# Selective scan of a two-layer convolution net: one scan instruction for two states, loops swapped, half sums kept, background work placed in half slots

## The chip, the cores and the metric

The kernel runs on one core of one Trainium2 chip, in float32 throughout. The metric is device microseconds of one launch, as a median over runs. The host only lays the arrays out.

## The reference, cut to what matters

Two layers, each added to its own input after a group norm. Layer 0 is a row recurrence (a masked convolution along a row and a gated state carried from row to row). Layer 1 takes each image of 96 channels through a wavelet split into 64x64 bands; the low band goes through a two-dimensional selective scan, the high bands through a channel attention, and a transposed convolution joins them again. The change lies in the selective scan:

```python
x_dbl = jnp.einsum('bkdl,kcd->bkcl', xs, x_proj_w)
dts, Bs, Cs = jnp.split(x_dbl, [DT_RANK, DT_RANK + D_STATE], axis=2)
delta = jax.nn.softplus(jnp.einsum('bkrl,kdr->bkdl', dts, dt_w) + dt_b[None, :, :, None])
A = -jnp.exp(A_logs).reshape(K, D_INNER, D_STATE)
def step(hst, inp):
    u_t, d_t, B_t, C_t = inp
    dA = jnp.exp(d_t[..., None] * A)
    hst = dA * hst + (d_t * u_t)[..., None] * B_t[:, :, None, :]
    y = jnp.einsum('bkdn,bkn->bkd', hst, C_t)
    return (hst, y)
```

There are 8 images, K = 4 directions (rows, columns, and both backwards), 192 channels, 16 states and 4096 positions. For each direction, channel and state a first-order recurrence runs over the 4096 positions, and the 16 states are summed with weights C into one output.

## The kernel before, in words

**Stages.** Layer 0 and a set-up come first. Then the wavelet analysis of image 0 runs alone. Then comes the scan stage, 3072 slots in a row, in which the scans of image b have beside them, as background, the analysis of image b+1 and the output and synthesis of image b-1. The output and synthesis of image 7 run alone at the end.

**A slot.** The positions are cut into 8 chunks of 512 (`CH`). One pass `p` holds two directions: 128 partitions are 64 channels of a row direction and 64 of a column direction, and `q` = 0..2 picks the channel group. A slot is one chunk, one channel group and a pair (`GN` = 2) of states; a chunk has 24 slots, with the channel group innermost, so three slots in a row share a tile `bct` with the rows B and C of the pair, broadcast by DMA to the partitions (`load_bc`, L928). In a slot:

- POOL makes `xb` = `du` x B, 1024 elements, three slots ahead (`product`, L937).
- ACT makes `da` = exp(delta x A), two instructions of 512 elements into PSUM (`decay`, L946). There are three such one-bank buffers.
- DVE runs two scans of 512 elements over `da` and `xb` (`scan`, L953), in place in `da`; each takes its starting state from a column of the tile `carry`.
- DVE multiplies the states with C into `hc`, two instructions of 512 (L1102), and ACT copies the last state into `carry` (L1104). In every sixth slot (`by_pool`) the scan writes into `xb` instead, and POOL does the multiplication (L1096).
- PE sums over the states: transposing matmuls with the identity add each `hc` into the group's accumulator `py`, one PSUM bank for each of the three groups (`add_up`, L970). After the chunk's last pair ACT copies `py` out (L1034). In the backward pass the forward sum `yf` is loaded and added by a matmul (L1009).

**Background.** Jobs are Python generators; each step names an engine, an estimated time, a least distance in slots from the step before, and resources (PSUM banks, short tiles). `write` emits the steps that are due. In a slot the steps of SP, PE and ACT are emitted after the first `decay` and ahead of the scans; the steps of DVE and POOL are emitted at the slot's end, behind `hc`:

```python
write(left, EARLY, full)     # SP, PE, ACT
for j in range(GN):
    scan(s, j, None if first else carry)
...                          # product, hc, carry copies
write(left, LATE, full)      # DVE, POOL
```

`pin` then fixes the order of the instructions on each engine as it was emitted. Many jobs have a chain of ACT steps whose result a DVE step of least distance 0 uses, so that both fall into one slot: `softplus` (L910 to L912, then L914 on DVE), `silu` (L617 to L619, then L622), `norm` (L592, then L595; L600 and L601, then L605) and the output (L846, then L848).

**Turned tiles.** The column directions need the image transposed. `turn_u`, `turn_y` and `turn_r` collect 32 rows or columns (`HALF`), and ACT's queue then writes them to DRAM in runs of 32 elements: `turned` (L685, L686), `flush` (L1000, L1001), and `columns` (L669).

Of the kernel before, what the change touches and what calls it, by code (L numbers as in the profile page):

```python
# [7 lines left out]
F32 = mybir.dt.float32  # L8
# [15 lines left out]
HALF = 32  # L24
# [3 lines left out]
NSHORT = 12  # L28
# [28 lines left out]
def forward_kernel(ctx: ExitStack, tc: tile.TileContext, i, out):  # L57
# [172 lines left out]
    with ExitStack() as s:  # L230
# [103 lines left out]
        bcp = s.enter_context(tc.tile_pool(name="bbc", bufs=3))  # L334
        sp = s.enter_context(tc.tile_pool(name="bs", bufs=2))
        psh = s.enter_context(tc.tile_pool(name="bpsh", bufs=3, space=PSUM))
        psy = s.enter_context(tc.tile_pool(name="bpsy", bufs=1, space=PSUM))
# [33 lines left out]
        for k in range(4):  # L371
            r, p, h0 = dtrow[k], k // 2, k % 2
            nc.sync.dma_start(onecol[r + 6:r + 7, h0:h0 + 1], one)
            for q in range(3):
                ds = slice(64 * ((q + h0) % 3), 64 * ((q + h0) % 3) + 64)
                hs = slice(64 * h0, 64 * h0 + 64)
                nc.sync.dma_start(dw[r:r + 6, p, q, hs], i["dt_wT"][k, :, ds])
                nc.sync.dma_start(dw[r + 6:r + 7, p, q, hs], i["dt_b"][k, ds, :].rearrange("d o -> o d"))
                nc.sync.dma_start(av[hs, p, q, :], i["A_logs"][k, ds, :])
        nc.scalar.activation(av, av, AF.Exp)  # L380
# [52 lines left out]
        turn_u = wp.tile([128, W2, HALF], F32, name="turn_u")  # L433
        turn_y = wp.tile([128, H2, HALF], F32, name="turn_y")
        turn_r = wp.tile([128, H2, HALF], F32, name="turn_r")

# [20 lines left out]
        class Job:  # L457
# [3 lines left out]
            def __init__(self, due, gen, after=(), take=(), give=(), urgent=0):  # L461
# [12 lines left out]
        free = dict(bank=2, short=NSHORT, raw=3, ph=2, wa=2)  # L474
        jobs = []
        now = [0]
# [4 lines left out]
        def write(left, engines, full):  # L481

            moved = True
            while moved:
                moved = False
                for job in list(jobs):
                    if job.due > now[0] or not all(a.done and a.at < now[0] for a in job.after):
                        continue
# [8 lines left out]
                    while not job.done:  # L497
                        eng, us, wait, take, give = job.next
                        if eng not in engines or now[0] < job.at + wait or not takes(take):
                            break  # L500
                        if us > left[eng] and left[eng] < full[eng]:
                            break
# [11 lines left out]
        def add(due, gen, after=(), take=(), give=(), urgent=0):  # L514
            job = Job(due, gen, after, take, give, urgent)
# [7 lines left out]
        def hasten(job):  # L523
            if not job.done:
# [4 lines left out]
        def drain(until):  # L529
# [4 lines left out]
            while not all(j.done for j in until):  # L534
                big = dict(SP=1e9, PE=1e9, ACT=1e9, DVE=1e9, POOL=1e9)
                write(dict(big), EARLY, big)
                write(dict(big), LATE, big)
# [4 lines left out]
        def analysis(b, begin, end):  # L542
# [7 lines left out]
            def bands(j, g):  # L550
# [6 lines left out]
                raw = io.tile([128, 9, W], F32, name="raw", bufs=3)  # L557
# [12 lines left out]
                for ty in range(2):  # L570
                    yield "PE", 2.6, (1 if ty == 0 else 0), (BANK if ty == 0 else NONE), NONE
                    if ty == 0:
                        pd = ps.tile([128, 8, W2], F32, name="pd", tag="mm")
                    for tx in range(3):
                        nc.tensor.matmul(pd, wa[:, 3 * ty + tx, :], ph[:, ty:ty + 8, tx:tx + W2],  # L575
                                         start=(ty == tx == 0), stop=(ty == 1 and tx == 2))
                yield "ACT", 1.7, 1, NONE, BANK + ("ph", "wa")
                pdf = pd.rearrange("p r w -> p (r w)")
                his = short("his")
                nc.scalar.activation(his[0:96], pdf[0:96], AF.Copy, accum_out=part[:, g, j:j + 1])  # L580
                nc.scalar.copy(lls[32 * (g % 3):32 * (g % 3) + 32], pdf[96:128])
# [32 lines left out]
            def silu(pre, name):  # L614
                yield "ACT", 1.85, 1, NONE, NONE
                e = short("e")
                nc.scalar.activation(e, pre, AF.Exp, scale=-1.0)  # L617
                nc.scalar.activation(e, e, AF.Ln, bias=1.0)
# [5 lines left out]
            def project(j, part_i):  # L624
# [3 lines left out]
                for t0 in range(0, 9, 3):  # L628
                    yield "PE", 2.6, (1 if t0 == 0 else 0), (BANK if t0 == 0 else NONE), NONE
                    if t0 == 0:  # L630
                        pc = ps.tile([128, 8, W2], F32, name="pc", tag="mm")
                    for tap in range(t0, t0 + 3):
                        ty, tx = divmod(tap, 3)
                        nc.tensor.matmul(pc, wc[:, tap, d0:d0 + 128], xp[:, r + ty:r + ty + 8, tx:tx + W2],  # L634
                                         start=(tap == 0), stop=(tap == 8))
# [3 lines left out]
                hl = 8 * j % HALF  # L639
# [16 lines left out]
            def x_proj(odr, rhs, at):  # L656
# [9 lines left out]
                for dst, src in ((bc_d[b][odr], bcs[bp.start:bp.start + 32]),  # L666
                                 (bc_d[b][odr + 2], bcs[bp.start + 32:bp.start + 64]),
                                 (dt_d[b][dp], bcs[dp])):
                    nc.scalar.dma_start(at(dst), src if odr == 0 else src.rearrange("p (w h) -> p w h", h=HALF))  # L669
# [5 lines left out]
            def columns(half, c):  # L675
                nw = 512 // HALF
# [3 lines left out]
                    lambda d: d.rearrange("r (w h) -> r w h", h=H2)[:, nw * c:nw * c + nw, HALF * half:HALF * half + HALF])  # L680

            def turned(half):
                yield "ACT", 0.68, 1, NONE, NONE
                dst = u_d[b][1].rearrange("d (w h) -> d w h", h=H2)[:, :, HALF * half:HALF * half + HALF]
                nc.scalar.dma_start(dst[0:128], turn_u)  # L685
                nc.scalar.dma_start(dst[128:192], turn_r[0:64])  # L686

# [27 lines left out]
            def conv(j):  # L715
# [3 lines left out]
                first = list(old) if j % 4 == 0 else []  # L719
# [8 lines left out]
                if j % 4 == 3:  # L728
                    group = [p for t in range(j - 3, j + 1) for p in rows[t]]
                    td = put(at(0.65), turned(j // 4), after=group)  # L730
                    cl = [put(at(0.7 + 0.1 * c), columns(j // 4, c), after=group, take=SHORT, give=SHORT)
                          for c in range(4)]
# [446 lines left out]
```

## Time and profile before

| what | value |
|---|---|
| median of 3 runs | 16440.75 us (16437.21 to 16448.39) |
| the profiled execution: its time, its span | 16478.75 us, 16477.0 us |
| DVE busy | 12537.6 us (76% of the span) |
| PE busy, granted clock | 12192.1 us (74%), 0.842 |
| POOL busy | 10069.3 us (61%) |
| ACT busy | 8640.4 us (52%) |
| DMA: bytes, packets, packets under 512 B | 2236.11 MB, 1879932, 744738 |
| first and last scan start | 3583.2 us and 15975.5 us |

Busy times are shares of the whole span, and the stages differ: layer 0 is set by PE, the scan stage is not. "Idle before" in a group's row is the time in which that engine had nothing running just before the group's instructions, and the releaser named is what ended the wait.

### The profile page before, as it was taken

Reading aid. Unit: us, or ns where it says so; the run is one execution under the profiler, and the core shown is the slowest. Engines: PE = TensorE matmul, PEld = TensorE weight load, DVE = VectorE, ACT = ScalarE, POOL = GpSimd, SP = SyncE. Lnnn points to the kernel's source line nnn. Section 1 sums busy time; section 2 is a strip of 40 time slices with the busy share of each in tenths; the row PEclk is TensorE's granted clock in tenths of the full one; section 3 lists DMA queues with packets and bytes.
Section 4 is the critical chain, followed back from the end, with each engine's and each line's share of the span. In section 5 each row is a group of like instructions: output and inputs, shape, how many; then the busy total and the mean of one; then the engine's idle time right before and its main releaser. Section 6 shows DMA issues by size and latency. Waiting matters only on the chain. (4 is left out here: it accounts for less than half of the span.)

```text
span 16477.0 us, 148859 instructions
## 1 busy us (share of the span) xinstructions
PE 12192.1 (74%) x42082; PEld 6635.8 (40%) x42082; DVE 12537.6 (76%) x14498; ACT 8640.4 (52%) x17217; POOL 10069.3 (61%) x5752
## 2 busy tenths in 40 slices
PE   2999999577766777777777677767777677766666
PEld 1444444234444444444444444444444444434432
DVE  4333333139999988998899889988998899889971
ACT  1444444246665655565566556655655566544540
POOL 1333333028777766776677667766777677777760
PEclk9999999778877888888888888888888888877766
DMA  7333332346767776777677767767776777676653
GB/s 166 70 70 70 71 70 56 78 99 156 161 137 152 169 156 142 161 166 156 142 169 162 151 149 161 164 147 155 167 156 147 154 164 165 142 147 141 145 117 75
DMA packets 1879932, 2236.11 MB, mean 136 GB/s; under 512 B 744738, under 2 KB 944867, under 8 KB 1878852
## 3 DMA queue, kind: packets, MB, share of 16 engines
q1 hardware_dynamic: 1260611, 2004.22, 56.3%
q10 hardware_dynamic: 618496, 222.37, 6.0%
q8 instruction: 338, 5.54, 0.1%
q14 instruction: 487, 3.98, 0.1%
HBM read 1859.05 MB, written 367.00 MB: 135 GB/s over the span
## 5 line engine op out<-in xcount | busy, mean ns | idle before, releaser
L937 POOL TENSOR_TENSOR xb<-du,bct 128x1024 f32<-128x1024 f32 x3072 | 7192.7, 2363 | 2295.5 <-DMA bct<-bc_d 1893.3
L953 DVE TENSOR_TENSOR_SCAN da<-da,carry,xb 128x512 f32<-128x512 f32 x4480 | 5507.1, 1269 | 395.1 <-ACT da L946 338.9
L946 ACT ACTIVATE da<-dl,av 128x512 f32<-128x512 f32 x6144 | 4196.8, 690 | 999.2 <-DVE hc L1102 430.4
L970 PE MATMUL py<-ident,hc 128*128 128x128 f32 x20480 | 3464.1, 319 | 1595.8 <-DVE hc L1102 1582.9
L970 PEld LDWEIGHTS py<-ident,hc 128*128 128x128 f32 x20480 | 2791.5, 164 | 2925.8 <-DVE hc L1102 2509.7
L1102 DVE TENSOR_TENSOR hc<-da,bct 128x512 f32<-128x512 f32 x5120 | 3234.7, 671 | 164.6 <-PE py L970 164.3
L1104 ACT COPY carry<-da 128x1 f32<-128x1 f32 x4480 | 694.6, 155 | 3039.9 <-DVE hc L1102 2859.5
L180 PE MATMUL pg<-hx,wq 128*128 128x512 f32 x4608 | 2019.9, 592 | 0.0
L970 PE MATMUL py<-ident,xb 128*128 128x128 f32 x4096 | 760.9, 347 | 1130.3 <-POOL xb L1096 1125.6
L797 PE MATMUL pd<-ph,wg 128*128 128x504 f32 (+1 forms) x2304 | 1176.9, 657 | 308.1 <-DMA ph<-ll_d 116.5
L180 PEld LDWEIGHTS pg<-hx,wq 128*128 128x128 f32 x4608 | 871.7, 189 | 1107.0 <-issue 1106.2
L1096 POOL TENSOR_TENSOR xb<-xb,bct 128x1024 f32<-128x1024 f32 x512 | 1203.0, 2350 | 155.2 <-DVE xb L953 119.2
L575 PE MATMUL pd<-ph,wa 128*128 128x512 f32 x2304 | 1151.8, 643 | 149.8 <-DMA raw<-x_d 111.9
L970 PEld LDWEIGHTS py<-ident,xb 128*128 128x128 f32 x4096 | 616.8, 179 | 1502.3 <-POOL xb L1096 1426.9
L953 DVE TENSOR_TENSOR_SCAN xb<-da,carry,xb 128x512 f32<-128x512 f32 x896 | 1100.0, 1262 | 129.3 <-ACT da L946 96.3
L634 PE MATMUL pc<-xp,wc 97*128 97x512 f32 x2304 | 1126.7, 631 | 45.8 <-ACT attn L705 16.8
L185 ACT ACTIVATE gate<-pg,gbias 32x512 f32<-32x512 f32 x768 | 523.5, 682 | 1184.8 <-PE pg L180 1184.7
L197 POOL TENSOR_TENSOR x1b<-xb,hx 96x512 f32<-96x512 f32 x256 | 301.7, 1179 | 1372.5 <-DVE hx L196 1126.8
L191 DVE TENSOR_TENSOR gate<-gate,gate 96x512 f32<-96x512 f32 x256 | 186.6, 729 | 842.1 <-ACT gate L185 842.1
L953 DVE TENSOR_TENSOR_SCAN da<-da,xb 128x512 f32<-128x512 f32 x640 | 749.5, 1211 | 96.2 <-ACT da L946 70.6
L797 PEld LDWEIGHTS pd<-ph,wg 128*128 128x128 f32 x2304 | 470.8, 216 | 830.7 <-issue 634.8
L575 PEld LDWEIGHTS pd<-ph,wa 128*128 128x128 f32 x2304 | 460.3, 211 | 652.8 <-issue 477.0
(168 smaller groups left out, 11918.4 us busy)
## 6 DMA issues: line engine op xcount, KB each, us to landing
bct<-bc_d SPq DMA_DIRECT2D x2048, 512.0 KB
raw<-x_d SPq DMA_DIRECT2D x384, 288.0 KB
xb<-in_x SPq DMA_DIRECT2D x64, 1536.0 KB
wa<-wa_d SPq DMA_DIRECT2D x192, 384.0 KB
xs<-in_x SPq DMA_DIRECT2D x64, 1024.0 KB
x_d<-x1b SPq DMA_DIRECT2D x792, 64.0 KB
du<-u_d SPq DMA_DIRECT2D x128, 384.0 KB
yf_d<-y ACTq DMA_DIRECT2D x192, 256.0 KB
```

The lines of the kernel that those rows point to most:

```text
L180: nc.tensor.matmul(pg[m], wq[:, tap, m, :], hk[:, r, bs, tap:tap + W], start=False, stop=(tap == 2))
L185: nc.scalar.activation(gg[32 * m:32 * m + 32], pg[m][96:128], AF.Tanh, bias=gbias[96:128, m:m + 1])
L575: nc.tensor.matmul(pd, wa[:, 3 * ty + tx, :], ph[:, ty:ty + 8, tx:tx + W2], start=(ty == tx == 0), stop=(ty == 1 and tx == 2))
L634: nc.tensor.matmul(pc, wc[:, tap, d0:d0 + 128], xp[:, r + ty:r + ty + 8, tx:tx + W2], start=(tap == 0), stop=(tap == 8))
L797: nc.tensor.matmul(pd[:, :, c0:c1], wgs[g][:, 3 * ty + tx, :], ph[:, ty:ty + 8, c0 + tx - 1:c1 + tx - 1], start=(k == 0 and tx == 1), stop ...
L937: nc.gpsimd.tensor_mul(xb, inputs[s // SLOTS][1][:, s % 3, :].unsqueeze(1).to_broadcast([128, GN, CH]), bcts[s // 3][:, 0:GN])
L946: nc.scalar.activation(da, inputs[s // SLOTS][0][:, q, :], AF.Exp, scale=av[:, p, q, n:n + 1])
L953: nc.vector.tensor_tensor_scan(h[:, ::st], da[:, ::st], xb[:, j, ::st], 0.0 if carry is None else carry[:, q, n:n + 1], ALU.mult, ALU.add)
L970: nc.tensor.matmul(py[:, 128 * t:128 * t + 128], hc[:, j, 128 * t:128 * t + 128], ident, is_transpose=True, skip_group_check=True, start=( ...
L1096: nc.gpsimd.tensor_mul(xb, xb, bct[:, GN:2 * GN])
L1102: nc.vector.tensor_mul(hc[:, j], da, bct[:, GN + j])
L1104: nc.scalar.copy(carry[:, q, n0 + j:n0 + j + 1], da[:, e:e + 1])
```

## The change

**Two states in one scan.** `da` becomes one tile of 2 x 512 elements in two PSUM banks, with two such tiles, and one scan instruction runs over all 1024. The recurrence must not run from the first state into the second, and the chunk's starting state must come in otherwise than as the instruction's initial value: the job `border` sets delta to 1e30 at the chunk's first position, so that the decay there is exp of a huge negative number, 0 (a floor of -60 on A_logs keeps A away from 0); and it makes `ac` = (true decay at that position) x carry, which POOL adds to `xb` at that position in every slot (a 128x2 addition). `hc` is one instruction of 1024, and the carry copy one of two elements.

**Loops swapped.** A pass is four slots (`PASS`) of one channel group with four successive pairs of states. A chunk is two halves of the states, each with three passes. `bct` has six buffers instead of three; a block is loaded once its last user, in the pass of group 2, has been emitted, so four loads come in four successive slots and then none for eight. POOL's slots are those of the remainders 0 and 4 of twelve, the same share as before.

**Half sums kept.** The accumulators are two instead of three. After the first half of the states ACT copies `py` to a tile `half`, and after the second half matmuls with the identity add it, and in the backward pass `yf`, to the accumulator.

**Background in half slots.** A slot has a call of `background` ahead of the scan and, outside POOL's slots, another ahead of `hc`; each call emits first the due steps of SP, PE and ACT, and then those of DVE and POOL. Distances of 1 and 2 now count half slots (3 and more are doubled), overspent budgets are carried to the next call, and PE's long steps are cut into single matmuls.

**Memory and order.** The turned tiles hold 16 rows (`TURN`), so each image has twice as many flushes, in runs of 16 elements; a follower of a flush waits 8 more slots. There are 10 short tiles instead of 12, two `raw` tiles instead of three, `delta` and `du` are tiles by group, and the output's two parts go one after the other with 6 short tiles instead of 8.

The core of the diff:

```diff
-HALF = 32
+TURN = 16
-NSHORT = 12
+NSHORT = 10
...
-        bcp = s.enter_context(tc.tile_pool(name="bbc", bufs=3))
+        bcp = s.enter_context(tc.tile_pool(name="bbc", bufs=6))
-        psh = s.enter_context(tc.tile_pool(name="bpsh", bufs=3, space=PSUM))
-        psy = s.enter_context(tc.tile_pool(name="bpsy", bufs=1, space=PSUM))
+        psh = s.enter_context(tc.tile_pool(name="bpsh", bufs=2, space=PSUM))
+        psy = s.enter_context(tc.tile_pool(name="bpsy", bufs=2, space=PSUM))
...
-                        if eng not in engines or now[0] < job.at + wait or not takes(take):
+                        if eng not in engines or now[0] < job.at + (wait if wait < 3 else 2 * wait) or not takes(take):
                             break
-                        if us > left[eng] and left[eng] < full[eng]:
+                        if left[eng] <= 0.05:
                             break
...
+        def border(ci, q):
+            b, p, c = chunks[ci]
+            e0 = edges(ci)[0]
+            yield "ACT", 0.25, 1, NONE, NONE
+            dl = inputs[ci, q][0]
+            if not is_first(ci):
+                ac = inputs[ci, q][2] = sp.tile([128, NS], F32, name="ac", bufs=6)
+                nc.scalar.activation(ac, av[:, p, q, :], AF.Exp, scale=dl[:, e0:e0 + 1])
+            yield "POOL", 0.4, 0, NONE, NONE
+            if not is_first(ci):
+                nc.gpsimd.tensor_mul(ac, ac, carries[b, p][:, q, :])
+            nc.gpsimd.memset(dl[:, e0:e0 + 1], 1e30)
...
+                nc.gpsimd.tensor_mul(xb, du.unsqueeze(1).to_broadcast([128, GN, CH]), bcts[k][:, 0:GN])
+                if ac is not None:
+                    e0 = edges(ci)[0]
+                    nc.gpsimd.tensor_add(xb[:, :, e0], xb[:, :, e0], ac[:, n0:n0 + GN])
...
+            da, xb, h = (t.rearrange("p j l -> p (j l)")[:, ::st]
+                         for t in (das[s], xbs[s], xbs[s] if by_pool(s) else das[s]))
+            nc.vector.tensor_tensor_scan(h, da, xb, 0.0, ALU.mult, ALU.add)
...
+            if r == 1 and s % PASS == PASS - 2:
+                for y in parts_y.pop((ci, q)):
+                    nc.tensor.matmul(pys[key], ident, y, start=False, stop=False, skip_group_check=True)
...
+        def background(**full):
+            for eng, us in full.items():
+                left[eng] = us + min(left.get(eng, 0), 0)
+            write(left, EARLY)
+            write(left, LATE)
+            now[0] += 1
...
             if by_pool(s - 2):
                 add_up(s - 2)
             if not by_pool(s - 1):
                 add_up(s - 1)
+            if s and not by_pool(s - 1) and not is_last((s - 1) // SLOTS):
+                pc, _, pq, _, pn = place(s - 1)
+                nc.scalar.copy(carries[chunks[pc][0], chunks[pc][1]][:, pq, pn:pn + GN], das[s - 1][:, :, edges(pc)[1]])
+            das.pop(s - 1, None)
+            decay(s + 1, 0)
+            if s and s % PASS == 0:
+                evacuate(s - 1)
...
             pool = by_pool(s)
+            background(SP=1e9, PE=1.1, ACT=0.9, DVE=0.7, POOL=1.3)
+            scan(s)
             product(s + 3)
+            decay(s + 1, 1)
...
             else:
+                background(SP=1e9, PE=1.1, ACT=0.9, DVE=0.7, POOL=1.3)
+                hc = sums[s] = sp.tile([128, GN, CH], F32, name="hc")
+                nc.vector.tensor_mul(hc, das[s], bct[:, GN:2 * GN])
+            if q == 2:
+                load_bc(kb + 6)
```

## The prediction

> **What bounds the kernel now.** I read the page's line of engine totals, then busy time by stage, the waits of DVE within the scan stage, and a stretch of the timeline with every engine. The stage row is one image of the scan stage, 1550 us (columns: length, busy PE, PE weight loads, DVE, ACT, POOL, clock, DMA share, GB/s):
>
> ```profile
> 6700.00:8250.00 1550.00, 1134.63 (x4425) 653.71 (x4424) 1404.56 (x1570) 906.47 (x1885) 1114.42 (x578) 0.84 0.72 156
> ```
>
> DVE is busy for 1404.56 of 1550 (91%), PE and POOL for 73% and 72%. The eight windows from 3580 to 15980 give DVE 11321 us busy and 1079 idle in 12400: DVE sets the scan stage, and whatever makes it wait costs its full length. What makes it wait today (window 5000 to 15500; total, times, longest):
>
> ```profile
> DVE da L953 <- ACT da L946: 353.2, 145, 12.8
> DVE hc L1102 <- PE py L970: 156.7, 61, 3.9
> DVE raw L803 <- PE pd L797: 116.8, 40, 10.1
> DVE dl L914 <- ACT carry L1104: 63.6, 53, 3.6
> DVE dl L914 <- ACT dl L912: 57.8, 30, 8.1
> DVE u L622 <- ACT e L619: 9.1, 12, 1.7
> ```
>
> Of note are the small ones: DVE's background steps, the last three, hardly wait for ACT. The timeline shows why (start, length, engine):
>
> ```profile
> 7999.88 2.46 DVE L953 TENSOR_TENSOR_SCAN da<-da,carry,xb 128x512 f32<-128x512 f32 x2
> 7999.89 0.69 ACT L946 ACTIVATE da<-dl,av 128x512 f32<-128x512 f32 x1
> 8000.52 0.58 ACT L617 ACTIVATE e<-pc 128x512 f32<-128x512 f32 x1
> 8001.13 0.63 ACT L618 ACTIVATE e<-e 128x512 f32<-128x512 f32 x1
> 8001.79 0.63 ACT L619 ACTIVATE e<-e 128x512 f32<-128x512 f32 x1
> 8002.25 1.26 DVE L1102 TENSOR_TENSOR hc<-da,bct 128x512 f32<-128x512 f32 x2
> 8002.95 0.16 ACT L1104 COPY carry<-da 128x1 f32<-128x1 f32 x1 [0.53 <-DVE hc L1102]
> 8003.15 0.69 ACT L946 ACTIVATE da<-dl,av 128x512 f32<-128x512 f32 x1
> 8003.43 0.68 DVE L622 TENSOR_TENSOR u<-pc,e 128x512 f32<-128x512 f32 x1
> 8004.03 2.45 DVE L953 TENSOR_TENSOR_SCAN da<-da,carry,xb 128x512 f32<-128x512 f32 x2
> 8006.39 1.26 DVE L1102 TENSOR_TENSOR hc<-da,bct 128x512 f32<-128x512 f32 x2
> 8007.58 2.45 DVE L953 TENSOR_TENSOR_SCAN da<-da,carry,xb 128x512 f32<-128x512 f32 x2
> ```
>
> ACT's chain runs from 8000.52 to 8002.42, beside the scans; DVE's step that needs it (L622) comes a second later, behind `hc`. Also to be seen: the pair of scans takes 2.36 from start to the next start (8004.03 to 8006.39), the pair of `hc` 1.19, and ACT's copy and decay wait for `hc`.
>
> **Part 1, shorter DVE work.** In the first chunks, where no carry is read, the pair starts 2.24 apart (3600.69 to 3602.93), so reading the starting state costs 0.12 a pair. For the fixed part of an instruction: L610 (96x64) takes 205 ns, L605 (96x512) 669, so 1.036 ns an element; an `hc` of 512 at 0.595 leaves 0.06. One scan of 1024 is then an estimated 2.24 - 0.06 = 2.18. Ends: 2.24 (nothing fixed saved) and 2.10 (0.14 saved, all of L610's time beyond its elements). I take 2.18, as scan and product run on one engine. With 2688 slots after a carry, 384 without, and 2560 `hc` pairs: 2688 x 0.18 + 384 x 0.06 + 2560 x 0.06 = 661 us less; 477 to 907 at the ends. [...]
>
> **Part 2, DVE's steps move ahead of ACT.** This decides. `background` emits ACT's chain and at once DVE's step of distance 0, in the first call ahead of the scan, in the second ahead of `hc`. ACT can't be early: with two `da` tiles, `decay(s+1, 0)` stands before the chain and needs the tile that `hc(s-1)` has just read. Counted from the end of `hc(s-1)`, when DVE is free: 0.03 signal, 0.20 carry copy (8002.95 to 8003.15), 0.63 decay (7999.89 to 8000.52), 1.90 chain, 0.03 signal: DVE waits 2.79 with the scan queued behind. In the second call the next decay (0.63) comes too, 3.42 in all, less the scan of 2.18: DVE waits 1.24 with `hc` queued behind, and PE's sums behind that. Of 22 calls in 12 slots 12 are first ones: 0.55 x 2.79 + 0.45 x 1.24 = 2.09. At a pass's end, every fourth slot, ACT's copy of `py` stands ahead as well and waits for PE's eight transposes (1.25, then 0.59): some 1.05 in a quarter of the slots, 0.26 on average. So 2.35 for each of 381 softplus steps (384 of L914, three before the stage) and 168 silu steps (192 of L622, 24 before): 1290 us. Chain L600, L601 (1.24 with its gap; L605 56 times): 2.13 or 0.58, 1.7 with pass ends, 95 us. Steps that wait for a square (L595 behind L592, L848 behind L846; 0.58; 56 + 112 times): 1.47 or nothing, 1.0 with pass ends, 168 us. Together 1553. Where the budget splits a chain over two calls, 0.6 less; in a third of 549, -110. Today's such waits (121 for L914, 22 for L622 and L595, scaled from 10500 to 12400) go: -170. Ends: all in second calls, no pass ends, 549 x 1.24 + 56 x 0.58 = 713; all in first ones, 549 x 3.05 + 56 x 2.39 + 168 x 1.73 = 2099. I take the mix, 1553 - 110 - 170 = +1273.
>
> In a stall PE, POOL and ACT catch up. Of today's 1079 idle, 223 (part 3) and 170 are accounted for; of the other 686 I take off a third: -229.
>
> **Part 3, flushes.** ACT's queue is blocked by them:
>
> ```profile
> L1001 ACTq DMA_DIRECT2D y_d<-turn_r x16: 7346/11002/15373, 4649.0 to 15985.9; - x16
> ```
>
> L686 is alike (median 8960). In the block at 5899.36 (10.05 us) DVE waited 7.74 for `da`; 29 blocks lie in the stage, x 7.7 = 223 today. After: 58 blocks. DVE then has the rest of its slot and one more, 1.1 + 3.3 = 4.4. If a block's time goes with its packets, whose number per flush stays, 58 x (10 - 4.4) = 325; if with its bytes, 58 x (5 - 4.4) = 35. I take 230, nearer to the first, since the rows show many small packets beside few bytes on ACT's queue (618496 packets, 222 MB): +7. [...]
>
> **Part 4, the rest.** Pass ends in POOL's slots: the second decay is ready at 0.03 + 0.20 + 0.63, `py` copied at 1.95, decay at 2.6, against a scan of 2.18 with no `hc`: 0.4 x 512 = 205, of which part was in the old wait for `da`: +100 (0 to 205). PE: 384 more additions at 1.02 (L1009, two instructions), 392 us, beside 27% idle. ACT: 2240 carry copies fewer (-347), 384 copies of half sums (+225), `border` (336 at 0.25, as L705: +84): nothing. SP: four `bct` loads in a burst, each behind an `hc`; the first is needed by POOL three slots on as today, and five `xb` tiles cover some 7 us more; without that cover 5 us in each of 256 bursts would be 1280. Head and tail (630 and 497 us) have fewer buffers and twice the flushes, uncovered: +50 (0 to 120).
>
> Sum: -661 + 1273 - 229 + 7 + 100 + 50 = +540. The profiled execution took 16479, so 17019; the median lies 38 lower: **16980 us**.
>
> **The rivals.** (A) Faster: ACT's chains don't hold DVE, because they fall into second calls or are split, or because ACT is ahead after all. For: today's placing hides them wholly. Against: the order of emission, and rows in which ACT waits for `hc`. With the low end, 713 - 170 = +543 in place of 1273: 16250. With none, and nothing caught up: -661 - 170 + 157 = -674, so 15770. It decides where the mean wait of the 773 steps is under (661 - 157 + 229 + 170) / 773 = 1.17 us. (B) Faster, but set by POOL: per 12 slots 12 products at 2.33, two products with copies 5.2 and 2.6 of background (L916, L833), now 12 x 7/8 additions at 0.2 (L916 1286 ns for 512, L937 2363 for 1024: 0.21 fixed) and 0.5 of `border`: 38.4, or 3.20 a slot; with today's wait for `bct` (1893 / 3072 = 0.62) 3.82, times 3072 = 11730 in place of 12400: about 15820. It is a floor under A. (C) The scan over two banks gains nothing over two scans: 507 back, 17490.
>
> **How the numbers follow.** The measurement tells 0.2% (33 us) from no change. The forecast has 0.60, its own range 16500 to 17500 (mean wait 1.3 to 2.6); A 0.25, B 0.06, C 0.04, and 0.05 lies within 0.2% between A and the forecast. Faster 0.31, same 0.05, slower 0.64. The range goes from 15950, which leaves out A with no stall at all and B, to 17450.
>
> **What would show it.** Right: L953 as 128x1024 at 2.2 to 2.3 us; the waits of DVE's background steps (those of L914, L622, L595, L605, L848 today) for ACT above 1000 us; DVE busy in the stage near 10660, idle near 2230; some 60 blocks of 8 to 10 us on ACT's queue. Wrong: those waits under 700 us, or POOL over 90% busy in the stage.

## The result: 18% slower, and where the time went

The kernel after takes 19460.79 us (median of 4 runs, 19451.76 to 19476.5) against 16444.57 (16437.21 to 16458.16): 1.1834 times as long, 95% interval 1.1814 to 1.1855, or 3016 us more. The forecast was 16980 with a range of 15950 to 17450. The direction was right, the size was not.

The profiled execution has a span of 19448.9 us (before 16477.0, so 2972 more). The scan stage by windows, first of the kernel before, then of the kernel after (columns as in the prediction), and the window 6700 to 8250 of the kernel after, which the prediction shows of before:

```profile
3580.00:15980.00 12400.00, 8838.98 (x34718) 5216.73 (x34718) 11321.29 (x12646) 7213.46 (x15043) 9073.98 (x4680) 0.82 0.71 154
```

```profile
3580.00:18900.00 15320.00, 9879.99 (x35411) 5710.74 (x35410) 10896.44 (x6996) 7236.05 (x13520) 9623.24 (x8068) 0.77 0.60 125
6700.00:8250.00 1550.00, 1007.81 (x3571) 570.12 (x3570) 1100.31 (x714) 725.97 (x1364) 964.70 (x824) 0.78 0.60 124
```

DVE's busy time falls by 425 us with 5650 instructions fewer, and its idle time rises from 1079 to 4424 (the last 48 us of the stage after lie behind this window). No other engine is full: POOL has 63% of the stage and PE 64%. So DVE waits, and the waits tell for what (window 5000 to 18500; total, times, longest):

```profile
DVE dl L946 <- ACT dl L944: 1029.5, 334, 8.9
DVE da L1018 <- ACT da L1005: 711.6, 253, 16.3
DVE raw L812 <- PE pd L806: 393.2, 109, 14.2
DVE u L629 <- ACT e L626: 303.8, 95, 14.8
DVE xb L1018 <- ACT carry L1143: 167.5, 19, 18.2
DVE da L1018 <- ACT carry L1143: 162.3, 23, 14.7
DVE uo L859 <- ACT t L857: 151.3, 56, 5.9
DVE xp L611 <- ACT pv L607: 121.2, 48, 4.0
DVE ysum L846 <- POOL ysum L844: 106.0, 35, 8.3
```

`dl` at L946 is the softplus step that was L914 before and waited 57.8 us for its own chain (63.6 more for `carry`); `u` at L629 was L622 with 9.1. The timeline has one such wait whole (start, length, engine; in brackets the idle time before it and its releaser):

```profile
8971.39 2.29 DVE L1018 TENSOR_TENSOR_SCAN da<-da,xb 128x1024 f32<-128x1024 f32 x1
...
8973.71 1.22 DVE L1187 TENSOR_TENSOR hc<-da,bct 128x1024 f32<-128x1024 f32 x1
...
8974.85 2.29 DVE L1018 TENSOR_TENSOR_SCAN da<-da,xb 128x1024 f32<-128x1024 f32 x1
...
8977.24 1.22 DVE L1187 TENSOR_TENSOR hc<-da,bct 128x1024 f32<-128x1024 f32 x1
...
8978.50 0.16 ACT L1143 COPY carry<-da 128x2 f32<-128x2 f32 x1 [1.86 <-DVE hc L1187]
...
8978.69 0.69 ACT L1005 ACTIVATE da<-dl,av 128x512 f32<-128x512 f32 x1
...
8979.65 0.58 ACT L1087 COPY half<-py 128x512 f32<-128x512 f32 x1 [0.27 <-PE py L1032]
8980.14 0.60 ACT L941 ACTIVATE dl<-pt 128x512 f32<-128x512 f32 x1
...
8980.77 0.63 ACT L943 ACTIVATE dl<-dl 128x512 f32<-128x512 f32 x1
8981.43 0.63 ACT L944 ACTIVATE dl<-dl 128x512 f32<-128x512 f32 x1
...
8982.09 0.69 DVE L946 SCALAR_TENSOR_TENSOR dl<-pt,dl 128x512 f32<-128x512 f32 x1 [3.62 <-ACT dl L944]
8982.70 2.29 DVE L1018 TENSOR_TENSOR_SCAN da<-da,xb 128x1024 f32<-128x1024 f32 x1
```

When `hc` ends (8978.46) ACT begins carry copy, decay, the copy of the half sums (which waits 0.27 for PE) and then the chain; DVE stands still 3.62 us with the next scan queued behind L946, although that scan's decays were long done.

ACT's queue, in a slot with a flush; the first fence is the timeline, the second the rows of the two flushes (min/median/max in ns). The issue at L692 occupies ACT's queue for 19.54 us, and DVE stands idle for 16.59 us until the next scan:

```profile
8997.31 2.29 DVE L1018 TENSOR_TENSOR_SCAN da<-da,xb 128x1024 f32<-128x1024 f32 x1
...
8998.23 19.54 ACTq L692 DMA_DIRECT2D u_d<-turn_r  x1
8999.50 0.67 DVE L812 TENSOR_TENSOR raw<-raw,pd 64x512 f32<-64x512 f32 x1
...
9018.61 2.29 DVE L1018 TENSOR_TENSOR_SCAN xb<-da,xb 128x1024 f32<-128x1024 f32 x1 [16.59 <-ACT carry L1143]
```

```profile
L692 ACTq DMA_DIRECT2D u_d<-turn_r x32: 4858/5981/21167, 3397.6 to 16875.6; - x32
L1071 ACTq DMA_DIRECT2D y_d<-turn_r x32: 4751/9094/16559, 4718.6 to 18956.2; - x32
```

The trace's idle stretches of DVE from the first scan to the end of the last, added up by the line that ends them, close the account. Stretches that end during a DMA issue of over 2.5 us on ACT's queue, or within 4 us behind it, have a row of their own; 59 of these 64 issues after, and 29 of 33 before, are flushes:

| us of DVE in the stage | before | after | change |
|---|---|---|---|
| work | 11316 | 10931 | -385 |
| idle beside long issues on ACT's queue | 215 | 541 | +326 |
| idle at steps that wait for ACT's chains and squares (L946, L629, L859, L611, L601) | 160 | 2028 | +1868 |
| idle at scans | 417 | 857 | +440 |
| idle at steps that wait for PE or POOL (L812, L846, L874, L881) | 121 | 733 | +612 |
| idle at `hc` | 164 | 214 | +50 |
| start of the first scan | 3583 | 3632 | +49 |

That is +2960 of the span's 2972.

### The profile page after: what moved, and what is told of

Read it like the earlier page. It is cut to its first block, busy times and chain, and to the rows that moved or that the text cites. A ratio compares the mean times of both kernels' runs of the same rounds, so it can differ in the third digit from the quotient of the medians.

```text
span 19448.9 us, 143663 instructions
## 1 busy us (share of the span) xinstructions
PE 13247.8 (68%) x42850; PEld 7147.5 (37%) x42850; DVE 12152.7 (62%) x8867; ACT 8663.7 (45%) x15697; POOL 10645.4 (55%) x9160
## 3 DMA queue, kind: packets, MB, share of 16 engines
q10 hardware_dynamic: 1143808, 222.38, 7.2%
q14 instruction: 433, 3.55, 0.1%
## 5 line engine op out<-in xcount | busy, mean ns | idle before, releaser
L1018 DVE TENSOR_TENSOR_SCAN da<-da,xb 128x1024 f32<-128x1024 f32 x2560 | 5859.1, 2289 | 1054.8 <-ACT da L1005 811.9
L1032 PE MATMUL py<-ident,hc 128*128 128x128 f32 x20480 | 3659.2, 338 | 3399.4 <-DVE hc L1187 3392.6
L1032 PEld LDWEIGHTS py<-ident,hc 128*128 128x128 f32 x20480 | 3022.1, 175 | 4898.5 <-DVE hc L1187 4068.9
L1187 DVE TENSOR_TENSOR hc<-da,bct 128x1024 f32<-128x1024 f32 x2560 | 3128.2, 1222 | 220.0 <-PE py L1032 36.6
L1143 ACT COPY carry<-da 128x2 f32<-128x2 f32 x2240 | 357.7, 160 | 4683.8 <-DVE hc L1187 4473.6
L806 PE MATMUL pd<-ph,wg 128*128 128x504 f32 (+1 forms) x2304 | 1306.7, 704 | 352.7 <-DMA ph<-ll_d 254.3
L580 PE MATMUL pd<-ph,wa 128*128 128x512 f32 x2304 | 1302.1, 701 | 332.8 <-ACT ph L574 289.4
L1018 DVE TENSOR_TENSOR_SCAN xb<-da,xb 128x1024 f32<-128x1024 f32 x512 | 1167.2, 2280 | 216.7 <-ACT carry L1143 169.3
L948 POOL TENSOR_TENSOR du<-du,dl 128x512 f32<-128x512 f32 x384 | 486.0, 1266 | 1151.8 <-DVE dl L946 1147.9
L946 DVE SCALAR_TENSOR_TENSOR dl<-pt,dl 128x512 f32<-128x512 f32 x384 | 265.5, 691 | 1215.5 <-ACT dl L944 1215.5
```

The source lines that it names most:

```text
L806: nc.tensor.matmul(pd[:, :, c0:c1], wgs[g][:, 3 * ty + tx, :], ph[:, ty:ty + 8, c0 + tx - 1:c1 + tx - 1], start=(k == 0 and tx == 1), stop ...
L948: nc.gpsimd.tensor_mul(du, du, dl)
L1018: nc.vector.tensor_tensor_scan(h, da, xb, 0.0, ALU.mult, ALU.add)
L1032: nc.tensor.matmul(pys[key][:, 128 * t:128 * t + 128], hc[:, j, 128 * t:128 * t + 128], ident, is_transpose=True, skip_group_check=True, s ...
L1187: nc.vector.tensor_mul(hc, das[s], bct[:, GN:2 * GN])
```

## The experiments

Every time is a median, every ratio is to the kernel before on the same chip, with its 95% interval. "After" is the changed kernel (19460.79).

**e1: DVE's and POOL's steps behind `hc` again.** In the kernel after, `background` emits only the steps of SP, PE and ACT; those of DVE and POOL come at the slot's end, as they did before.

```diff
             write(left, EARLY)
-            write(left, LATE)
...
                 nc.vector.tensor_mul(hc, das[s], bct[:, GN:2 * GN])
...
+            for eng, us in dict(DVE=0.7 if pool else 1.4, POOL=1.3 if pool else 2.6).items():
+                left[eng] = us + min(left.get(eng, 0), 0)
+            write(left, LATE)
```

> The changed kernel with one thing put back: the due steps of DVE and POOL are emitted at the slot's end, behind hc, as in the kernel before; SP, PE and ACT keep their two calls a slot. Theory 1 (DVE's steps stand ahead of the scan or of hc and hold DVE while ACT runs their chain): the some 2190 us of waits at L946, L629, L859, L611 and L601 fall below 500, and the time from 19461 to 17400 us (17100 to 17700). Theory 2 (ACT and PE are simply late, by flushes and by half-slot distances): the waits move to the scans, and the time stays above 18800.

17788.98 us, 1.0826 [1.0805, 1.0846]: 1672 less than after, a little above the range of theory 1 (17700) and far below theory 2. The waits of DVE (window 5000 to 16800):

```profile
DVE da L1018 <- ACT da L1005: 801.7, 284, 15.8
...
DVE dl L946 <- ACT carry L1141: 221.4, 77, 11.9
...
DVE dl L946 <- ACT dl L944: 72.5, 47, 5.9
```

The wait of L946 for its own chain (`dl` L944) falls from 1029.5 to 72.5; by the same sums as in the table all waits at L946 go from 1182 to 210, and L812's from 394 to 55. Some of it comes back elsewhere: idle time beside long issues rises from 541 to 753, at `hc` from 214 to 314. More than half of the loss is this order of emission.

**e4: the same order in the kernel before.** One line moves, nothing else of the change is made.

```diff
             write(left, EARLY, full)
+            write(left, LATE, full)
             for j in range(GN):
                 scan(s, j, None if first else carry)
...
-            write(left, LATE, full)
```

> The kernel before with one thing changed: the due steps of DVE and POOL are emitted right behind those of SP, PE and ACT, ahead of the slot's scans. Theory 1 (placement): each of 549 chains holds DVE some 2.8 us, 56 by 2.1 and 168 by 1.5, 1900 less today's 170: 18150 us (17700 to 18500). Theory 2 (placement is harmless, the scan's new form or the DMA runs cost the time): 16450 to 16700.

18475.86 us, 1.1236 [1.122, 1.1253]: 2045 more than before. Its waits (window 5000 to 17500) are those of the kernel after, at the kernel before's lines:

```profile
DVE dl L914 <- ACT dl L912: 1158.0, 328, 17.3
DVE u L622 <- ACT e L619: 327.1, 96, 5.9
DVE uo L848 <- ACT yk L846: 269.4, 110, 5.3
```

With e1 this shows from both sides that the place of these steps is the largest cause.

**e3: the flushes in long runs.** The turned tiles go to DRAM as they lie, in runs of 4 KB (16 x 64 elements) in place of 64 bytes; the kernel leaves out turning them, so the order in DRAM is wrong. The edit at L692's flush is alike.

```diff
-            dst = y_d[b][1].rearrange("d (h w) -> d h w", w=W2)[:, :, w0:w0 + TURN]
+            dst = y_d[b][1][:, H2 * w0:H2 * (w0 + TURN)].rearrange("d (h w) -> d h w", w=TURN)
```

> The changed kernel with the flushes of the turned tiles written in runs of 4 KB to the same regions, without turning them back: the same bytes in far fewer packets, the order of the data in DRAM is left wrong. Theory (the runs of 64 bytes block ACT's queue): the 60 blocks go, DVE's loss beside them (540 us) falls below 120, the time to 19000 (18850 to 19150). Rival (blocks lie in time that DVE waits anyway): above 19350.

18945.76 us, 1.1524 [1.1507, 1.1541]: 515 less than after. The same issue with the same bytes:

```profile
L1071 ACTq DMA_DIRECT2D y_d<-turn_r x32: 452/460/1812, 4685.3 to 18460.4; - x32
```

So the blocking goes with the pieces into which the bytes are cut, not with the bytes: the queue's packets go from 1143808 to 369664 at 222.38 MB (64 flushes of 192 rows, each row 64 pieces of 64 bytes after and one of 4 KB here). The blocks' part of the idle time falls from 541 to 118 in the sums.

**e2: two scans in the same tile.** Scan and `hc` are two instructions of 512 each, on the one tile of two banks.

```diff
-            nc.vector.tensor_tensor_scan(h, da, xb, 0.0, ALU.mult, ALU.add)
+            for j in range(GN):
+                da, xb, h = (t[:, j, ::st] for t in (das[s], xbs[s], xbs[s] if by_pool(s) else das[s]))
+                nc.vector.tensor_tensor_scan(h, da, xb, 0.0, ALU.mult, ALU.add)
```

> The changed kernel with each scan of 1024 as two scans of 512 (both start from 0, as border gives the start) and hc as two products of 512. Theory (a product that reads what the scan just before it wrote waits for the scan to drain: scan to product is 2.39 us in the trace, where scan to another step is 2.2): the two halves hide this, 2.24 + 1.19 = 3.43 a slot against 3.53, so 230 us less: 19230 (19100 to 19350). Rival (one instruction saves its fixed cost, as the prediction had it): 5632 instructions more by 0.06 us, 340 us more: 19800.

19372.78 us, 1.1784 [1.1766, 1.1801]: 88 less, where 230 were expected. Splitting alone gains little as long as both halves are one tile:

```profile
9035.75 2.50 DVE L1018 TENSOR_TENSOR_SCAN da<-da,xb 128x512 f32<-128x512 f32 x2 [1.98 <-ACT da L1005]
9038.35 1.29 DVE L1188 TENSOR_TENSOR hc<-da,bct 128x512 f32<-128x512 f32 x2
```

The product starts 2.60 us behind the first scan, and by the sums DVE's work grows by 602 us while its idle time falls by 678.

**e5: two tiles of one bank.** `da` is two tiles; the scans still start from 0 (`border` stays), and each state has its own carry copy.

```diff
-                    das[s] = psh.tile([128, GN, CH], F32, name="da")
+                das.setdefault(s, []).append(psh.tile([128, CH], F32, name="da", bufs=4))
...
+            for j in range(GN):
+                da, xb = das[s][j][:, ::st], xbs[s][:, j, ::st]
+                nc.vector.tensor_tensor_scan(xb if by_pool(s) else da, da, xb, 0.0, ALU.mult, ALU.add)
```

> The changed kernel with the two-state scan alone undone: da is two tiles of one bank again, with two scans of 512 from 0 (border keeps the start), two products and two carry copies; slots, loops, background as changed. Theory (a product right behind the scan whose tile it reads starts 2.39 us after it, not 2.2; two tiles hide that, and they free da half by half, so that ACT starts some 0.6 us earlier): 3.43 a slot in place of 3.53, 256 us, and some 390 us of waits for ACT: 18820 (18550 to 19150). Rival (the fixed cost of 5632 more instructions decides, as predicted): 19800. Third (like the run with two scans in one tile): 19370.

18666.32 us, 1.136 [1.1343, 1.1377]: 794 less than after. A slot of DVE in the timeline:

```profile
9004.50 2.32 DVE L1017 TENSOR_TENSOR_SCAN da<-da,xb 128x512 f32<-128x512 f32 x2
9006.73 1.27 DVE L1190 TENSOR_TENSOR hc<-da,bct 128x512 f32<-128x512 f32 x2
9007.92 2.33 DVE L1017 TENSOR_TENSOR_SCAN da<-da,xb 128x512 f32<-128x512 f32 x2
```

The product starts 2.23 us behind the first scan. Slot to slot it takes 3.42 us with four instructions, against 3.46 (8971.39 to 8974.85 above) and a median of 3.53 over the trace with two. Over the stage little of the 794 is this: by the sums DVE's work rises by 128 us, and its idle time at `hc` falls by 134. What falls is time that DVE waits behind ACT: 428 in place of 857 idle at scans, 1815 in place of 2028 at the steps behind ACT's chains, 442 in place of 541 beside long issues. ACT has the first of the two tiles back some 0.6 us sooner; that this is the reason is read from the order of emission, not tried by itself.

**e8: the starting state alone, in the kernel before.** All scans start from 0.

```diff
-                                         0.0 if carry is None else carry[:, q, n:n + 1], ALU.mult, ALU.add)
+                                         0.0, ALU.mult, ALU.add)
```

> The kernel before with every scan started from 0, so that the state isn't carried from chunk to chunk; all else is kept, the carry copies too. Measures what the start column costs. Theory (0.12 us a pair, from 2.36 and 2.24 in the trace of before, in 2688 slots, all of it on the path): 320 us less, 16110 (16050 to 16200). Rival (DVE waits for others, and what is saved turns into waiting): 16350 or more.

16259.4 us, 0.9896 [0.9879, 0.9912]: 168 less than before, half of what was expected (the kernel leaves out the state carried from chunk to chunk). A scan falls from 1269 to 1210 ns and DVE's work by 288, but its idle time rises from 1077 to 1148.

**e9, e6, e7, e10, e12: the edits together.** e9 is e1 with e5's two tiles; e6 is e1 with e3's flushes; e7 is e1 with all distances in whole slots; e10 is e1, e5 and e3; e12 adds e7's edit to e10:

```diff
-                        if eng not in engines or now[0] < job.at + (wait if wait < 3 else 2 * wait) or not takes(take):
+                        if eng not in engines or now[0] < job.at + 2 * wait or not takes(take):
```

> The changed kernel with two things put back: DVE's and POOL's steps at the slot's end, and da as two tiles with two scans. Theory (the causes add up: 1672 for the place of the steps, 794 for the two-state scan): 17000 (16900 to 17250). Rival (the two tiles help only the chains that stand ahead of the scan, by letting ACT start earlier, and these are gone): 17600 or more.

17434.08 us, 1.0613 [1.0597, 1.0628]: 355 less than e1, where e5 was worth 794 alone: between its theory and its rival. Part of e5's gain was in the waits that e1 takes away too.

> The changed kernel with DVE's and POOL's steps at the slot's end and with the flushes in runs of 4 KB (order in DRAM left wrong). In the run with the steps at the slot's end, DVE lost 753 us beside long issues on ACT's queue. Theory (the two causes add up): 600 less than 17789, 17180 (17000 to 17350). Rival (with the steps late, ACT's blocks are covered): above 17600.

17292.55 us, 1.0524 [1.0508, 1.054]: 496 less than e1; the flushes cost about the same in both orders.

> The changed kernel with DVE's and POOL's steps at the slot's end and with all distances in whole slots again (twice the half slots). Theory 3 (ACT's steps at a distance of a half slot wait for PE and hold the decays, 917 us of waits at the scans outside the flushes against 417 in the kernel before): 17250 (17000 to 17450). Rival (the two da tiles, not the distances, make the decays late): 17700 or more.

17708.47 us, 1.0776 [1.076, 1.0792]: 81 less than e1. The theory that the half-slot distances matter much falls.

> As the run before it, with the flushes in runs of 4 KB besides (order in DRAM left wrong). Theory (three causes, 1672 + 794 + 515, are nearly the whole 3016 of the change): 16480 (16400 to 16700). Rival (half of what is left has another cause: half-slot distances, fewer tiles, the bursts of loads): 16900 or more.

17001.59 us, 1.0351 [1.0334, 1.0369]. The theory falls here too: 577 us above the kernel before are left.

> The kernel after with four edits: DVE's and POOL's background steps at the slot's end, two one-bank da tiles with two scans each, flushes in runs of 4 KB (DRAM order left wrong), and every distance of the background counted in whole slots. Without the last edit the run took 17001.59, some 570 us above the kernel before. Theory: with the other three causes gone, what is left of DVE's waits in the scan stage (120 for POOL at ysum and its neighbours, part of 162 at u, 139 at xp, part of 284 at dl, and scans behind a crowded ACT) comes from the half-slot distances, so whole slots win about 300 us: 16700 (16550 to 16800). Rival: distances are worth as little as they were beside the one-tile scan (80 us): 16920 (16850 to 17000), and the rest lies in the passes' ends (copies of half sums waiting for PE) and in the column runs that the 4 KB edit does not touch.

16975.02 us, 1.0329 [1.0312, 1.0346], 27 less than e10, and the two intervals overlap: the rival holds, and the distances are out.

**e14 and e13: the copies at the passes' ends a slot later.** In the kernel after, ACT waits there for PE (waits of ACT, window 5000 to 18500):

```profile
ACT y L1094 <- PE py L1032: 439.2, 311, 7.0
ACT half L1087 <- PE py L1032: 253.6, 292, 8.8
```

The edit emits these copies one slot later, except at a chunk's end:

```diff
-            if s and s % PASS == 0:
+            if s and s % SLOTS == 0:
                 evacuate(s - 1)
+            elif s % PASS == 1 and s % SLOTS > 1:
+                evacuate(s - 2)
```

e14 is the kernel after with this edit alone, e13 is e12 with it.

> The kernel after with the one edit that ACT's copy of a pass's sums is emitted one slot later. The prediction put 0.26 us of each of some 549 chains (143 us) and 100 us of the scans' waits on the copies at the passes' ends. Theory: that much goes, 19220 (19100 to 19320). Rival: the chain of softplus or silu is late for other reasons, and the copies cost under 80 us: 19400 (19380 to 19480).

18967.45 us, 1.1536 [1.1518, 1.1553]: 493 less than after, twice the theory. The waits of ACT (window 5000 to 18000) keep one of the two rows; the other is not among its first rows any more:

```profile
ACT y L1094 <- PE py L1032: 133.1, 118, 5.3
```

DVE's idle at scans goes from 857 to 350 in the sums, that at L946 only from 1182 to 1078: it is the second decay behind the copy that was late, not the chains.

> All four edits (background of DVE and POOL at the slot's end, two one-bank tiles, flushes in runs of 4 KB with the DRAM order left wrong, whole-slot distances; 16975.02, some 545 above before) and ACT's copy of a pass's sums (y, half) emitted one slot later, when PE has them. In the window 5000 to 15500 ACT waits 530 us for PE at y and 484 at half, against 302 at y before. Theory: these waits hold the decays and the background's chains behind them and are worth 250 us: 16725 (16550 to 16850). Rival: ACT has room for them, and the rest lies elsewhere: 16930 (16880 to 17000).

16611.48 us, 1.0104 [1.0089, 1.0119]: 364 less than e12 and 175 above the kernel before. With the order, the one-tile scan, the flushes and the copies undone (and the distances, which are worth little) 94% of the loss (2849 of 3016) is gone. But e13 keeps the change's gain too, the scans that start from 0: beside e11 below, which has that gain without the rest, about 390 us are left.

**e15 and e16: one call of `background` a slot.** e15 is e12, e16 is e13, each with the first call alone and the budgets of before; that also halves DVE's and POOL's budgets outside POOL's slots (0.7 in place of 1.4, 1.3 in place of 2.6).

```diff
-            background(SP=1e9, PE=1.1, ACT=0.9)
+            background(SP=1e9, PE=1.4 if pool else 2.6, ACT=0.7 if pool else 1.9)
             scan(s)
...
-                background(SP=1e9, PE=1.1, ACT=0.9)
                 hc =
```

> All four edits, and the background in one call a slot, with the budgets of the kernel before (PE 1.4 in POOL's slots or 2.6, ACT 0.7 or 1.9, DVE 0.7, POOL 1.3): ACT's steps all ahead of the scan, and at most about one step of DVE in a slot's end. Theory: the second call puts ACT's steps between the two decays, and two DVE steps in a row behind hc wait for each other's inputs; without it 200 us go: 16775 (16600 to 16880). Rival: the placing within the slot no longer matters once DVE's steps stand behind hc: 16960 (16900 to 17050).

> Both further edits on top of the four (one call a slot, copies of the sums a slot later). If both theories hold, 16525 (16350 to 16700), within 100 us of the kernel before; if neither does, 16900 or above, and what is left of the 545 us lies in what these edits keep: fewer buffers, half sums, column runs of 64 bytes, and POOL's border steps.

e15 17093.55 us, 1.0397 [1.0382, 1.0413], 118 more than e12; e16 16967.88, 1.0324 [1.0307, 1.0341], 356 more than e13. The theory falls with the sign turned. Whether the second call or the larger budget is worth having, the two edits do not tell apart, and why the two differ by 238 was not tried.

**e11: what is good in the change, alone.** In the kernel before all scans start from 0, with the true carry brought in: per chunk and group ACT makes `ac`, and POOL adds `ac` x carry to the first column of `xb` in every slot, two 128x2 steps. The loads of `bct` also wait for the analysis of their image.

```diff
+                ac = inputs[s // SLOTS][3]
+                if ac is not None:
+                    q, n0 = s % 3, GN * (s % SLOTS // 3)
+                    e0 = 0 if chunks[s // SLOTS][1] == 0 else CH - 1
+                    ax = sp.tile([128, GN], F32, name="ax")
+                    nc.gpsimd.tensor_mul(ax, ac[:, q, n0:n0 + GN], carry[:, q, n0:n0 + GN])
+                    nc.gpsimd.tensor_add(xb[:, :, e0], xb[:, :, e0], ax)
...
-                                         0.0 if carry is None else carry[:, q, n:n + 1], ALU.mult, ALU.add)
+                                         0.0, ALU.mult, ALU.add)
```

> The kernel before with one part of the change alone, kept whole: scans start from 0, and the chunk's start comes in through xb at the first position (ac = decay there, made once a chunk and group by ACT; ac x carry and the addition, two 128x2 steps on POOL in every slot); loads of bct wait in the order of work for the analysis. Theory (the start column cost 168 us in the run that left the carry out, and POOL has room for 0.4 us more a slot): 16270 (16200 to 16350), faster than both. Rival (POOL's additions make xb late): 16450 or more.

16212.65 us, 0.9869 [0.9854, 0.9884]: faster than both kernels, and 212 us (1.3%) below the one before. Its stage by windows, and the scan's row:

```profile
3580.00:15700.00 12120.00, 8709.46 (x34668) 5187.52 (x34669) 10932.58 (x12629) 7260.85 (x15366) 9978.57 (x10049) 0.83 0.70 157
```

```profile
L967 DVE TENSOR_TENSOR_SCAN da<-da,xb 128x512 f32<-128x512 f32 x5120 | 5990.6, 1211 | 412.7 <-ACT da L960 345.0
```

DVE's busy time is 389 us below before's, nearly the whole reduction of the kernel after (425), and its idle time is 1187, 108 more than before. POOL's 905 us more are hidden beside DVE.

## Why the prediction was wrong, step by step

The forecast's total was +540 of the profiled execution, the profile shows +2972. Its mechanism, DVE waiting in order for ACT, was right. What failed are the sizes of its terms. Of the 2432 us between the two, part 1 with the idle time at `hc` is 326 (-335 in place of -661), the steps named in part 2 are 595, the steps that it did not list 612, idle time at scans 569 (+440 in place of -229 and +100), the long issues 319, and 11 are the small rest.

**Part 1, forecast -661; work -385, and some 180 of it given back.** The rows of the scan and of `hc` after:

```profile
L1018 DVE TENSOR_TENSOR_SCAN da<-da,xb 128x1024 f32<-128x1024 f32 x2560 | 5859.1, 2289 | 1054.8 <-ACT da L1005 811.9
L1187 DVE TENSOR_TENSOR hc<-da,bct 128x1024 f32<-128x1024 f32 x2560 | 3128.2, 1222 | 220.0 <-PE py L1032 36.6
```

The estimate of 2.18 for the scan is nearly reached only when something else follows: L812 starts 2.19 behind the scan at 8997.31 (medians over the trace 2.20 for L846, but 2.31 for L812), while `hc` starts 2.32 and 2.39 behind the scans at 8971.39 and 8974.85, and the median over the trace's slots is 2.39. So 214 us stand idle before `hc`, only 37 of them for PE; before, nearly all of the 164 were for PE. Before, a second scan lay between a scan and the product of its state. The step that failed is that the scan's time was read off pairs whose order was interleaved: a slot of scan and `hc` takes 3.53 against 3.55 before (medians), where 3.31 was forecast. The saving that fewer instructions were to bring by themselves (0.06 each) does not show either: with four instructions on two tiles (e5) such a slot takes 3.43. So rival C's mechanism held (two states in one scan gain nothing), and most of what is left of part 1 is the missing starting state, which e8 and e11 show without the rest.

**Part 2, forecast +1273; +1868, and +612 that was not listed.** The steps named were the right ones, and e1 and e4 show the cause. The mean wait was put at 2.35; L946's is 3.12 (1182 us, 379 waits outside flushes). The price of a first call was right: the trace has 90 such waits with no copy of `py` in or just before them, 2.58 in the mean (forecast 2.79), and 169 with one, 3.92 (forecast 2.79 + 1.05; the timeline's 3.62 is one). Three other figures were wrong: 259 of 379 are first calls, 68% where 55% was taken; a copy stands ahead in nearly half of all waits, not in a quarter; and the 120 in second calls wait 2.40, not 1.24, for which no single reason was tried. The list was short as well: DVE's early steps that wait for PE or POOL (L812, L846, L874, L881) were left out because only ACT's chains were counted; they cost 733 where 121 was, and e1 takes L812 from 394 to 55. Rival A, decided by a mean wait under 1.17, was far off.

**ACT's start behind `hc`** was read off rightly from before. The row of ACT's waits has it (at `carry` 2457.4 us before, window 5000 to 15500, and 3976.3 after, window 5000 to 18500): `carry` copies a column that the scan finished, yet waits for `hc`, which only reads the same tile (1.86 us at 8978.50), and starts 0.03 us after `hc` ends (median of the 2240 copies after). What makes one reader wait for the other was not tried.

**Part 3, forecast +7 (230 in place of 223); +326 (541 in place of 215).** e3 gives 515 and e6 496 for all the flushes' blocks after, where 230 was taken. I took the block's time to fall with its bytes in part, and a longer slot to cover 4.4 of it. But a flush of half the bytes takes 5981 of 8960 ns (L692 against L686) and 9094 of 11002 (L1071 against L1001) in the median, up to 21167, and the mean over the stage's 59 is 10.6 us, no less than the 10.0 of the 29 before. DVE idles 8.6 us beside each, where 4.0 was taken (7.2 before): neither the shorter block nor the longer cover is there. With the packets of a flush as before, a time that goes with them would make the same bytes in runs of 64 take 2 times as long as in runs of 128, one that goes with the bytes 1 time. The rows give 2 x 5981 / 8960 = 1.34 and 2 x 9094 / 11002 = 1.65 by medians; by the means in the stage (11.59 against 9.14 us at L692, 9.61 against 10.84 at L1071) it is 2.54 and 1.77. The end of 325, in which the time goes with the packets, was nearer to the 541 of the sums than the 230 taken, though still too low.

**The catch-up, forecast -229, has the wrong sign, and the passes' ends, forecast +100, were five times as dear.** In a stall ACT, PE and POOL did not run ahead: what DVE's scans wait for (`da` from ACT) comes out of the same in-order queue in which ACT waits for DVE (the 3976.3 us at `carry`) and, at each pass's end, for PE (439.2 and 253.6 us at `y` and `half`). Idle at scans rose by 440; with the copies `half` and `y` moved (e14) 507 of the 857 go, and 493 us of the time. Their price was taken as 0.4 for each of POOL's slots, while the trace has the second decay held behind them at any pass's end: it starts 2.24 us after the first where such a copy alone lies between (median of 485 slots), 0.72 where nothing does.

**Rival B** (POOL's floor) is out: 9623 of 15320 us. Head and tail were forecast at +50, and the first scan starts 49 later. Of the other terms' own ends only that of part 2 (2099 for the steps named) holds what was measured (2028). The far ends of part 1 (477 saved), of the flushes (325) and of the passes' ends (205) were all passed. They were read from a kernel in which DVE hardly waits; in the kernel after each stall also delays what ACT can begin only behind `hc`. That reading is argued from the rows, not tried.

Singly, e1, e3, e5 and e14 give back 1672 + 515 + 794 + 493 = 3474, more than the 3016 lost, so they overlap; together (e13) they give 2849. The last 175 us, or some 390 beside e11, are open. The waits of DVE in e13 (window 5000 to 15500):

```profile
DVE hc L1191 <- PE py L1031: 282.8, 145, 4.2
DVE ysum L846 <- POOL ysum L844: 224.9, 53, 10.4
DVE da L1017 <- ACT da L1004: 175.5, 98, 4.9
DVE raw L812 <- PE pd L806: 162.4, 30, 12.2
DVE u L629 <- ACT e L626: 115.8, 24, 8.5
```

`hc` waits longest, for PE (156.7 in the kernel before); the two accumulators in place of three, the column runs of 64 bytes at L675, the smaller number of short tiles and POOL's border steps are still in it; none of these was tried alone.

## What to carry to other kernels

On an engine that sets the time, what counts is what stands in front of its own work in the queue: a background step belongs behind the instruction that gives its producer time, and moving it ahead can cost more than a shorter instruction saves (here 2045 us in e4, beside the 385 us of work that the change saves). Before merging two instructions, see what now directly follows on the result, and which other engine gets its buffer back later. List every step of the moved kind with its producer, whatever engine that is, and let the upper ends of terms that share a queue add up.

## What the runs showed of the hardware

- After, a product that reads what the scan just before it wrote starts 2.39 us (median) after the start of a scan of 1024, L846 in that place 2.20 and L812 2.31: 0.08 to 0.19 us in a slot.
- A starting state read from a tile costs a scan of 512 about 59 ns (1269 before, 1210 in e8).
- An issue of a flush in runs of 64 bytes holds ACT's queue for up to 21.2 us (L692 after); the same bytes in runs of 4 KB take 0.46 to 0.48 in the median (e3).
- The granted clock was 0.842 before, where PE stood idle 1596 us before its matmuls on `hc`, and 0.802 after, with 3399. These 20480 matmuls took 319 ns each before and 338 after. Whether the idle time lowers the clock, and what the lower clock adds to DVE's waits for PE, was not tried.
